# Two of seven quadrant products, done once more as seven products of quarters

## The chip, the cores and the metric

The kernel is written for one core of a Trainium2 chip. A core has a matrix engine (TensorE, PE in the profile; its weight loads are shown apart, as PEld), a vector engine (VectorE, DVE), an activation engine (ScalarE, ACT), a general engine (GpSimd, POOL), and SyncE (SP), whose queue issues most of the transfers between the chip's main memory and the core's memory. The engines run side by side, each in the order of its own queue, and wait for one another by semaphores. TensorE writes its results to PSUM, a small memory of banks; DVE and ACT read them from there. The metric is the device time of one execution, in microseconds; lower is better.

## The reference

The reference is four layers, one after the other, on eight 512x512 float32 matrices: a grid stencil, a transformer block with attention, a gated expert and a low-rank response. The change touches two feed-forward layers, that of the transformer block and that of the expert:

```python
# transformer block
h = _ln(x) * g2 + beta2
ff = _gelu2(h @ W1 + b1) @ W2 + b2
return x + ff
# expert
h = jax.nn.gelu(jnp.einsum('bsh,bhi->bsi', input_tensor, Wi_b) + bi_b[:, None, :], approximate=False)
o = jnp.einsum('bsi,bih->bsh', h, Wo_b) + bo_b[:, None, :]
r = o + input_tensor
```

For each of the eight matrices both are a product 512x512 by 512x2048, a GELU, and a product 512x2048 by 2048x512, whose result is added to the layer's input.

## The kernel before

The last stage, `mlp_stage` (L1237), runs 16 passes, q = 0 to 15: passes 0 to 7 are the transformer's feed-forward for the eight matrices, passes 8 to 15 the expert's. The hidden width of 2048 is cut into four groups g of 512, so a pass is four 512x512 products in its first layer and four, added up, in its second.

Each 512x512 product is cut into 2x2 quadrants of 256 and done by the Strassen-Winograd scheme: seven products of quadrants in place of eight, at the price of sums and differences of quadrants. For the first layer the sums of the weights are made by `w_quads` (L1573) and those of the input by `b_quads` (L1543). For the second layer the sums of the activations (left side) are made on DVE by `s13`, `t2s2`, `t4s4`, those of the weights wo (right side) on POOL by `t13` (L1738), `t2s2`, `t4s4`. A quadrant product of the second layer is `second` (L1672): for each of the four groups four matmuls that load 128x128 weights and stream 256 columns, all 16 added up in one PSUM bank.

The order is written out by hand. A pass has 56 steps of four matmuls each: steps 0 to 27 are the first layer (seven products for each group), steps 28 to 55 the second: p1 from step 28, p5 from 32, p2 from 36, p6 from 40, p3 from 44, p7 from 48, p4 from 52. A table `hooks` says which other work is issued before which step (`at`, L1958); `go(s)` inside `run` (L1599) issues it. Each engine keeps the order in which its work was issued. So a hook sets the place in every queue, not the time: an engine that is ahead does the work earlier than the step's matmuls, one that is behind does it later.

Hooks that matter here: the loads (`load_wi` L1406, `load_wo` L1419, `load_x`) on SP's queue; `w_quads` of groups 2 and 3 of the same pass at steps 7 and 14 and of groups 0 and 1 of the next at 46 and 50, on POOL; `add_row` (L1456), a 128x2048 addition on POOL at step 2; `norm` at 29 and `b_quads` of the next pass at 51, on DVE; in passes 0 to 7 four steps of a Gram-Schmidt loop (`gs_b`, L1313) at 4, 18, 40 and 53, each of which goes from DVE to POOL (a square root), back to DVE, and ends with two small transfers from POOL's queue (`gs_a`, L1302) that the next step waits for; in passes 9 to 15 the tail of the pass before (normalization, spread through main memory, response).

Buffers: a tile pool hands out a fixed number of buffers under each tag, in turn; a new tile waits until the last reader of the old one in its buffer is done. Tags x0 to x3 hold the first layer's weights (one buffer of 128x2048 each, one for each group), wo0 to wo3 those of the second layer, act0 to act3 the activations, and six PSUM banks (tag u) go round among all products. In pass 15, p4 is done in two halves by rows, each followed by `last_row` (L1873), with the last normalization between them.

Of the kernel before, what the change touches and what calls it, by code (L numbers as in the profile page):

```python
# [11 lines left out]
F32 = mybir.dt.float32  # L12
# [4 lines left out]
ALU = mybir.AluOpType  # L17
# [1219 lines left out]
def mlp_stage(tc, a, small, xp, io, wo8, x1d, ident, eidx, sigs, layernorm, rstd_of, phalf, wl3, g2, b1, first):  # L1237
# [19 lines left out]
    with ExitStack() as ctx:  # L1257
# [160 lines left out]

        def load_wo(q):  # L1419
            one = expert(q) if q >= NB else None  # L1420
            wos[q] = {}
            for g in range(NG):
                t = wp.tile([P, KC, D], F32, name=f"wo_{q}_{g}", tag=f"wo{g}", bufs=1)
                if q < NB:
                    load_w2(nc, t, a, g)
                else:
                    nc.sync.dma_start(
                        t,
                        a["Wo_e"][one, g * D : (g + 1) * D, :].rearrange(
                            "o (j p) d -> p (o j) d", p=P  # L1430
                        ),
                    )
                wos[q][g] = t

        def load_extra(q):

# [162 lines left out]
        def run(q, hooks):  # L1599
            def go(s):  # L1600
                for f in hooks.get(s, []):
                    f()

            func = AF.Gelu_apprx_sigmoid if q < NB else AF.Gelu
            bi = b1 if q < NB else extra[q][0]
            x = xs[q]
            acts, ss = {}, {}

            def act_quad(g, i, j):

                return acts[g][:, 2 * j : 2 * j + 2, H * i : H * i + H]

            def s13(g):
                ss[g] = io.tile([P, 2, H], F32, name=f"s_{q}_{g}", tag=f"v{g}", bufs=2)
                add(ss[g], act_quad(g, 1, 0), act_quad(g, 1, 1))
                add(act_quad(g, 1, 0), act_quad(g, 0, 0), act_quad(g, 1, 0), ALU.subtract)

            for g in range(NG):
                acts[g] = ap.tile([P, KC, D], F32, name=f"act_{q}_{g}", tag=f"act{g}", bufs=1)
                out = {  # L1620
                    (i, j): acts[g][:, 2 * i : 2 * i + 2, H * j : H * j + H]
                    for i in range(2) for j in range(2)
                }

                def gelu(i):
                    for k in (2 * i, 2 * i + 1):
                        j = 4 * g + k
                        pin(
                            nc.scalar.activation(  # L1629
                                acts[g][:, k, :], acts[g][:, k, :], func, bias=bi[:, j : j + 1]  # L1630
                            )
                        )

                p = []
                for m, (an, bn) in enumerate(L1):
                    go(7 * g + m)
                    A, B = wss[q, g][an], tbs[q][bn]
                    u = ps.tile([P, 2, H], F32, name=f"u_{q}_{g}_{m}", tag="u", bufs=6)
                    for i in range(2):
                        for k in range(2):  # L1640
                            mm(
                                as_rows(u, B(k))[i], A[:, k, i * P : (i + 1) * P], B(k),
                                i == 0 and k == 0, i == 1 and k == 1,
                            )
                    p.append(u)
                    if m == 0:
                        u1 = ap.tile([P, 2, H], F32, name=f"u1_{q}_{g}", tag="tmp", bufs=4)
                        pin(nc.scalar.copy(u1, p[0]))  # L1648
                    elif m == 1:
                        add(out[0, 0], p[1], u1)  # L1650
                    elif m == 2:
                        u2 = ap.tile([P, 2, H], F32, name=f"u2_{q}_{g}", tag="tmp", bufs=4)
                        add(u2, p[2], u1)
                        if g:
                            s13(g - 1)
                    elif m == 3:
                        u3 = ap.tile([P, 2, H], F32, name=f"u3_{q}_{g}", tag="tmp", bufs=4)
                        add(u3, p[3], u2)
                    elif m == 4:
                        add(out[1, 1], p[4], u3)  # L1660
                        add(u2, p[4], u2)
                    elif m == 5:
                        add(out[1, 0], p[5], u3)
                        gelu(1)
                    elif m == 6:
                        add(out[0, 1], p[6], u2)
                        gelu(0)

            wo, ts = wos[q], {}
            tvs = extra["t", q]  # L1670

            def second(s, A, B, each=None):  # L1672
                y = ps.tile([P, 2, H], F32, name=f"y_{q}_{s}", tag="u", bufs=6)
                for g in range(NG):
                    go(s + g)
                    if s == 28 and g == 2:
                        s13(NG - 1)
                    for i in range(2):
                        for m in range(2):
                            mm(  # L1680
                                y[:, m, :], A(g)[:, i, m * P : (m + 1) * P], B(g)[:, i, :],
                                g + i + m == 0, g + i + m == NG + 1,
                            )
                    if each:
                        each(g)
                return y

            def x_add(i, j, t):
                o = quad(x, i, j)
                add(o, t, o)  # L1690

            def b(i, j):
                return lambda g: quad(wo[g], i, j)

            yu = ap.tile([P, 2, H], F32, name=f"yu_{q}", tag="yu", bufs=1)

            def t2s2(g):
                gadd(tvs[g], quad(wo[g], 1, 1), tvs[g], ALU.subtract)
                add(ss[g], ss[g], act_quad(g, 0, 0), ALU.subtract)

            def t4s4(g):
                gadd(quad(wo[g], 1, 0), quad(wo[g], 1, 0), tvs[g], ALU.subtract)
                add(act_quad(g, 0, 1), act_quad(g, 0, 1), ss[g], ALU.subtract)

            p1 = second(28, lambda g: act_quad(g, 0, 0), b(0, 0))
            pin(nc.scalar.copy(yu, p1))
            x_add(0, 0, p1)
            p5 = second(32, lambda g: ss[g], lambda g: tvs[g], t2s2)
            x_add(1, 1, p5)
            x_add(0, 1, p5)  # L1710
            p2 = second(36, lambda g: act_quad(g, 0, 1), b(1, 0), t4s4)
            x_add(0, 0, p2)
            p6 = second(40, lambda g: ss[g], lambda g: tvs[g])
            add(yu, p6, yu)
            x_add(0, 1, yu)
            p3 = second(44, lambda g: act_quad(g, 0, 1), b(1, 1))
            x_add(0, 1, p3)
            p7 = second(48, lambda g: act_quad(g, 1, 0), b(0, 1))
            add(yu, p7, yu)
            x_add(1, 1, yu)  # L1720
            x_add(1, 0, yu)
            if q < NQ - 1:
                p4 = second(52, lambda g: act_quad(g, 1, 1), b(1, 0))
                x_add(1, 0, p4)
            else:
                for m in range(2):
                    y = ps.tile([P, H], F32, name=f"y_{q}_52_{m}", tag="u", bufs=6)
                    for g in range(NG):
                        if g % 2 == 0:
                            go(52 + 2 * m + g // 2)  # L1730
                        for i in range(2):
                            mm(
                                y, act_quad(g, 1, 1)[:, i, m * P : (m + 1) * P],
                                b(1, 0)(g)[:, i, :], g + i == 0, g + i == NG,
                            )
                    last_row(m, y)

        def t13(q, g):  # L1738

            w = wos[q][g]  # L1740
            t = io.tile([P, 2, H], F32, name=f"t_{q}_{g}", tag=f"v{g}", bufs=2)
            gadd(t, quad(w, 0, 1), quad(w, 0, 0), ALU.subtract)
            gadd(quad(w, 0, 1), quad(w, 1, 1), quad(w, 0, 1), ALU.subtract)
            extra.setdefault(("t", q), {})[g] = t
# [223 lines left out]
        for q in range(NQ):  # L1968
            hooks = {}
            nx = q + 1 if q + 1 < NQ else None  # L1970

            at(hooks, 0, load_wo, q)
            if nx:
                if nx >= NB:
                    at(hooks, 45, load_extra, nx)
                at(hooks, 2, load_x, nx)
                for g in range(NG):
                    at(hooks, 7 * (g + 1), load_wi, nx, g)
            if 1 <= q <= NB:
                at(hooks, 4, lambda q=q: nc.sync.dma_start(x2d[q - 1], xs[q - 1]))  # L1980

# [5 lines left out]
            if nx:  # L1987
# [9 lines left out]
                        at(hooks, 46 + c, scale, nx, c)  # L1997
                at(hooks, 51, b_quads, nx)
                at(hooks, 46, w_quads, nx, 0, gadd)
                at(hooks, 50, w_quads, nx, 1, gadd)  # L2000
            if q < NB:
                for i, s in enumerate((4, 18, 40, 53) if q else (18, 24, 40, 53)):
                    at(hooks, s, gs_b, 4 * q + i)
# [118 lines left out]
```

## Time and profile before

| what | us |
|---|---|
| median of three runs | 2673.83 (2673.12 to 2674.03) |
| the profiled execution's own time | 2672.99 |
| its span, first to last instruction | 2671.2 |
| PE busy | 2629.2 |
| DVE busy | 1879.8 |
| POOL busy | 1484.6 |
| ACT busy | 1008.3 |

The page is one execution under the profiler. Busy time is the union of an engine's instructions; the difference of span and busy time is when it stood still. A group is a line of the kernel, an engine, an operation, the tiles written and read (out<-in), shapes and a count. L1265 is the helper `mm`, through which every matmul of the last stage goes, so groups there are told apart by their tiles: u are the products of the first layer, y those of the second. The last stage begins at 1075.7 us and ends with the span; its passes 1 to 7 start 96.69 us apart, passes 9 to 14 about 100.3 to 100.9.

### The profile page before, as it was taken

The page shows a single profiled execution, that of the slowest core. Times are in us where ns is not written, and L with a number is a line of the kernel's source. Part 1 is how long each engine was busy: PE and PEld are TensorE (multiplying, and loading weights), DVE is VectorE, ACT ScalarE, POOL GpSimd, SP SyncE. Part 2 cuts the span into 40 slices and gives each one's busy share as a digit, 9 for nine tenths or more (in the row PEclk, how much of TensorE's full clock was granted, in tenths as well). Part 3 has the DMA queues.
Part 4 walks back from the last instruction along what each step waited for, and adds up shares of the span by engine and source line. Part 5 has one row for each costly group of instructions (what it writes and reads, how often), then busy time and mean ns, then how long its engine had stood idle before and what let it go on. Part 6 is the DMA issues. An engine that isn't in the chain of part 4 may idle for free.

```text
span 2671.2 us, 39378 instructions
## 1 busy us (share of the span) xinstructions
PE 2629.2 (98%) x14152; PEld 1950.0 (73%) x14152; DVE 1879.8 (70%) x3436; ACT 1008.3 (38%) x2100; POOL 1484.6 (56%) x1099
## 2 busy tenths in 40 slices
PE   6999999999999999999999999999999999999998
PEld 3455555555555555888888888888888888888887
DVE  7978888888888656666656656666466676676675
ACT  2676767677777765211211211210111221221221
POOL 4556565556555664565556565655635545545543
PEclk9999999999999999999999999999999999999999
DMA  9775766666666554653454454445345445445331
GB/s 332 251 233 191 249 214 228 214 244 236 202 239 218 189 167 151 197 148 98 149 148 133 134 145 151 111 141 163 107 140 172 138 151 178 136 149 181 123 105 37
DMA packets 241817, 460.31 MB, mean 172 GB/s; under 512 B 33905, under 2 KB 77497, under 8 KB 232535
## 3 DMA queue, kind: packets, MB, share of 16 engines
q1 hardware_dynamic: 237754, 447.04, 49.4%
q0 software_dynamic: 3552, 10.72, 3.0%
q8 instruction: 113, 1.85, 0.3%
q14 instruction: 82, 0.66, 0.1%
q10 hardware_dynamic: 316, 0.03, 0.0%
HBM read 398.43 MB, written 55.09 MB: 170 GB/s over the span
## 4 chain that ended last, share of the span: by engine, by line
PE 94%; DVE 3%; DMA 1%; ACT 1%; SPq 0%; issue 0%; POOL 0%; DVEq 0%; POOLq 0%; ACTq 0%
PE u L1265 29%; PE y L1265 28%; PE tr L593 9%; PE s L590 6%; PE ctx L590 4%; PE o L590 4%; PE pv L590 4%; PE pk L590 4%; PE pq L590 4%; PE xtr L593 1%; PE xb L593 1%; DMA a<-in_A 0%; DMA bt<-td 0%; DVE bt L1058 0%; PE po L1265 0%
## 5 line engine op out<-in xcount | busy, mean ns | idle before, releaser
L1034 POOL TENSOR_TENSOR bt<-bt,mk 128x1024 f32<-128x1024 f32 x256 | 541.9, 2141 | 56.8 <-DMA bt<-in_bias 45.6
L1265 PE MATMUL y<-wo,act 128*128 128x256 f32 x2560 | 566.3, 380 | 0.0
L1265 PEld LDWEIGHTS y<-wo,act 128*128 128x128 f32 x2560 | 484.5, 190 | 71.6 <-issue 6.7
L1063 ACT ACTIVATE bt<-bt,mn 128x512 f32<-128x512 f32 x512 | 365.8, 718 | 77.7 <-DVE mn L1058 77.6
L593 PEld LDWEIGHTS tr<-ident,bt 128*128 128x128 f32 x2048 | 229.3, 141 | 149.3 <-issue 102.1
L1058 DVE CUSTOM_DVE_ANT_0 bt<-s,bt 128x512 f32<-128x512 f32 x512 | 329.9, 684 | 4.9 <-PE s L590 4.3
L1265 PE MATMUL u<-bt,wi 128*128 128x256 f32 x1440 | 330.5, 379 | 0.0
L1271 DVE TENSOR_TENSOR act<-u,u 128x512 f32<-128x512 f32 x256 | 173.1, 683 | 200.7 <-PE u L1265 132.5
L1265 PEld LDWEIGHTS u<-bt,wi 128*128 128x128 f32 x1440 | 273.5, 190 | 37.2
L1090 ACT COPY pt<-tr 128x512 f32<-128x512 f32 x376 | 207.9, 585 | 207.0 <-PE tr L593 199.2
L593 PE MATMUL tr<-ident,bt 128*128 128x128 f32 x2048 | 276.2, 277 | 7.7 <-ACT pt L1090 3.3
L1265 PE MATMUL u<-tb,ws 128*128 128x256 f32 x1024 | 242.2, 379 | 0.0
L1265 PE MATMUL y<-t,s 128*128 128x256 f32 x1024 | 227.8, 380 | 0.0
L1274 POOL TENSOR_TENSOR t<-wo,t 128x512 f32<-128x512 f32 x64 | 107.4, 1702 | 203.0 <-PE y L1265 203.0
L1265 PEld LDWEIGHTS u<-tb,ws 128*128 128x128 f32 x1024 | 194.3, 190 | 26.6 <-DVE tb L1271 0.2
L1265 PEld LDWEIGHTS y<-t,s 128*128 128x128 f32 x1024 | 194.0, 190 | 26.1
L1629 ACT ACTIVATE act<-act,b 128x512 f32<-128x512 f32 x128 | 82.9, 711 | 292.8 <-DVE act L1271 292.8
L1088 DVE COPY pt<-tr 128x512 f32<-128x512 f32 x136 | 93.7, 689 | 139.8 <-PE tr L593 139.3
L1629 ACT ACTIVATE act<-act,bi 128x512 f32<-128x512 f32 x128 | 83.8, 712 | 282.6 <-DVE act L1271 282.6
L1648 ACT COPY u<-u 128x512 f32<-128x512 f32 x64 | 36.4, 569 | 397.0 <-PE u L1265 275.9
L1271 DVE TENSOR_TENSOR x<-y,x 128x512 f32<-128x512 f32 (+1 forms) x97 | 64.7, 680 | 155.1 <-PE y L1265 104.7
L1271 DVE TENSOR_TENSOR u<-u,u 128x512 f32<-128x512 f32 x192 | 130.9, 682 | 55.4 <-PE u L1265 55.2
(331 smaller groups left out, 4179.8 us busy)
## 6 DMA issues: line engine op xcount, KB each, us to landing
bt<-in_bias SPq DMA_DIRECT2D x256, 512.0 KB
wo<-in_W SPq DMA_DIRECT2D x32, 1024.0 KB
wi<-in_Wi SPq DMA_DIRECT2D x32, 1024.0 KB
wo<-in_Wo_e SPq DMA_DIRECT2D x32, 1024.0 KB
wi<-in_W SPq DMA_DIRECT2D x28, 1024.0 KB
td<-tt SPq DMA_DIRECT2D x22, 1024.0 KB
bt<-td SPq DMA_DIRECT2D x176, 128.0 KB
gq<-coef_q SPq DMA_DIRECT2D x21, 512.0 KB
```

The costliest lines, as they stand in the source:

```text
L590: pin(nc.tensor.matmul(out, lhsT=lhsT, rhs=rhs, start=start, stop=stop))
L593: pin(nc.tensor.transpose(out, src, ident))
L1034: nc.gpsimd.tensor_tensor(bt, bt, mask[b, r][:, None, :].to_broadcast([P, 2, S]), ALU.add)
L1058: nc.vector.tensor_tensor_reduce(bt[:, i, :], ss[h], bt[:, i, :], -1.0, 3.0e38, ALU.add, ALU.min, mn)
L1063: nc.scalar.activation(bt[:, i, :], bt[:, i, :], AF.Exp, bias=mn, scale=-1.0, accum_out=sums[b, c][:, h, r : r + 1],)
L1088: pin(nc.vector.tensor_copy(pt[:, :, r % 2, :], tr))
L1090: pin(nc.scalar.copy(pt[:, :, r % 2, :], tr))
L1265: pin(nc.tensor.matmul(out, lhsT=lhsT, rhs=rhs, start=start, stop=stop))
L1271: pin(nc.vector.tensor_tensor(out, x, y, op))
L1274: pin(nc.gpsimd.tensor_tensor(out, x, y, op))
L1629: nc.scalar.activation(acts[g][:, k, :], acts[g][:, k, :], func, bias=bi[:, j : j + 1])
L1648: pin(nc.scalar.copy(u1, p[0]))
```

## The change

The products p7 and p4 of the second layer are cut once more. Each is, over the four groups, a product of 256x1024 by 1024x256; its operands are seen as 2x2 quarters of 128 (with the groups side by side as a third dimension), and the same scheme is used on the quarters: seven products of quarters, each four matmuls (one for each group) that load 128x128 and stream 128 columns. `quarters` sets up the operands and their sums: four left sums on DVE, four right sums on POOL, 128x512 each, one of each in place and three of each in new homes. `third` issues the 28 matmuls into two PSUM banks, four products in the first and three in the second, and adds the products up: one copy on ACT and three sums on DVE after the first bank, one sum after the second, into a tile in the core's memory that then stands where the PSUM bank of p7 or p4 stood. In pass 15 only p7 is cut.

The homes of the sums are the buffers x1, x2 and x3, in which the first layer's weights of groups 1 to 3 are no longer needed from step 28 on. They are in use until the end of p7 (x1) and p4 (x2, x3), so the loads of the next pass move: group 0 at step 21 (was 7), group 1 at step 52 (was 14), groups 2 and 3 at step 0 of the next pass, ahead of its `load_wo` (were 21 and 28). `w_quads` of group 1 moves from step 50 to step 1 of the next pass. The right sums of p7 are at steps 28 to 31, its left sums at 40 to 43; the left sums of p4 at 44 to 47, its right sums at 41 to 44 (from pass 9 on all at step 40). The four activation tiles become one, and the four wo tiles become one, so that a quarter of all four groups can be taken with one access.

```diff
         def load_wo(q):
-            wos[q] = {}
+            wos[q] = wp.tile([P, NG, KC, D], F32, name=f"wo_{q}", tag="wo", bufs=1)
             for g in range(NG):
-                t = wp.tile([P, KC, D], F32, name=f"wo_{q}_{g}", tag=f"wo{g}", bufs=1)
+                t = wos[q][:, g]
...
+            acts = ap.tile([P, NG, KC, D], F32, name=f"act_{q}", tag="act", bufs=1)
...
+            def quarters(key, i, j, wi_, wj, homes):
+                def left(k, m):
+                    o = H * i + P * m
+                    return acts[:, :, 2 * j + k, o : o + P]
+                def right(k, n):
+                    o = H * wj + P * n
+                    return wo[:, :, 2 * wi_ + k, o : o + P]
+                s1, s2, s4, t1, t2, t4 = homes
+                L, M = left, right
+                four[key] = dict(
+                    a=((L(0, 0), M(0, 0)), (s2, t2), (L(0, 1), M(0, 1)), (s1, t1)),
+                    b=((L(1, 0), M(1, 0)), (s4, M(1, 1)), (L(1, 1), t4)),
+                )
+                sub = ALU.subtract
+                of_left = [
+                    lambda: add(s1, L(0, 1), L(1, 1)), lambda: add(s2, s1, L(0, 0), sub),
+                    lambda: add(L(0, 1), L(0, 0), L(0, 1), sub), lambda: add(s4, L(1, 0), s2, sub),
+                ]
+                of_right = [
+                    lambda: gadd(t1, M(0, 1), M(0, 0), sub), lambda: gadd(M(0, 1), M(1, 1), M(0, 1), sub),
+                    lambda: gadd(t2, M(1, 1), t1, sub), lambda: gadd(t4, M(1, 0), t2, sub),
+                ]
+                return of_left, of_right
+            def quarter_homes(n):
+                for k in range(1, 4)[n:]:
+                    t = xp.tile([P, KC, D], F32, name=f"q4_{q}_{k}", tag=f"x{k}", bufs=1)
+                    homes[k] = [t[:, c, :].rearrange("p (g d) -> p g d", g=NG) for c in range(KC)]
+            def third(s, key):
+                jobs = [
+                    (n, k, g, v) for n in "ab" for k, v in enumerate(four[key][n]) for g in range(NG)
+                ]
+                ys = {
+                    n: ps.tile([P, 4, P], F32, name=f"y_{q}_{s}{n}", tag="u", bufs=6) for n in "ab"
+                }
+                w = ap.tile([P, 4, P], F32, name=f"yw_{q}_{s}", tag="tmp", bufs=4)
+                y = ys["a"]
+                for i, (n, k, g, (A, B)) in enumerate(jobs):
+                    if i % 7 == 0:
+                        go(s + i // 7)
+                    last = len(four[key][n]) - 1
+                    mm(
+                        ys[n][:, k, :], A[:, g, :], B[:, g, :], k + g == 0,
+                        k == last and g == NG - 1,
+                    )
+                    if n == "a" and k == last and g == NG - 1:
+                        pin(nc.scalar.copy(w[:, 0, :], y[:, 0, :]))
+                        add(w[:, 1, :], y[:, 1, :], w[:, 0, :])
+                        add(w[:, 2, :], y[:, 2, :], w[:, 1, :])
+                        add(w[:, 1:4:2, :], y[:, 3:4, :].to_broadcast([P, 2, P]), w[:, 1:3, :])
+                add(w[:, 0:3, :], ys["b"][:, 0:3, :], w[:, 0:3, :])
+                return w.rearrange("p (m n) d -> p m (n d)", m=2)
...
+            l7, r7, l4, r4 = early_quarters()
+            for i, f in enumerate(r7):
+                at(hooks, 28 + i, f)
+            for i, f in enumerate(l7):
+                at(hooks, 40 + i, f)
+            if q < NQ - 1:
+                for i, f in enumerate(l4):
+                    at(hooks, 44 + i, f)
+                for i, f in enumerate(r4):
+                    at(hooks, 41 + i if q <= NB else 40, f)
...
-            p7 = second(48, lambda g: act_quad(g, 1, 0), b(0, 1))
+            p7 = third(48, "p7")
...
-                p4 = second(52, lambda g: act_quad(g, 1, 1), b(1, 0))
+                p4 = third(52, "p4")
...
+            if q:
+                at(hooks, 0, load_wi, q, 2)
+                at(hooks, 0, load_wi, q, 3)
+                at(hooks, 1, w_quads, q, 1, gadd)
             at(hooks, 0, load_wo, q)
...
-                for g in range(NG):
-                    at(hooks, 7 * (g + 1), load_wi, nx, g)
+                at(hooks, 21, load_wi, nx, 0)
+                at(hooks, 52, load_wi, nx, 1)
...
-                at(hooks, 50, w_quads, nx, 1, gadd)
```

More of the change, by code (lines that the diff above doesn't have):

```diff
@@ L1432, in load_wo @@
                     )
-                wos[q][g] = t
         def load_extra(q):
@@ L1606, in run @@
             x = xs[q]
-            acts, ss = {}, {}
+            ss = {}
+            acts = ap.tile([P, NG, KC, D], F32, name=f"act_{q}", tag="act", bufs=1)
             def act_quad(g, i, j):
-                return acts[g][:, 2 * j : 2 * j + 2, H * i : H * i + H]
+                return acts[:, g, 2 * j : 2 * j + 2, H * i : H * i + H]
             def s13(g):
@@ L1618, in run @@
             for g in range(NG):
-                acts[g] = ap.tile([P, KC, D], F32, name=f"act_{q}_{g}", tag=f"act{g}", bufs=1)
                 out = {
-                    (i, j): acts[g][:, 2 * i : 2 * i + 2, H * j : H * j + H]
+                    (i, j): acts[:, g, 2 * i : 2 * i + 2, H * j : H * j + H]
                     for i in range(2) for j in range(2)
@@ L1629, in gelu @@
                             nc.scalar.activation(
-                                acts[g][:, k, :], acts[g][:, k, :], func, bias=bi[:, j : j + 1]
+                                acts[:, g, k, :], acts[:, g, k, :], func, bias=bi[:, j : j + 1]
                             )
@@ new lines, in run @@
+            four = {}
+            homes = {}
+            def quarter_homes(n):
[26 more added lines that the diff above has]
+                return w.rearrange("p (m n) d -> p m (n d)", m=2)
@@ L1688, in x_add, with early_quarters @@
+            def early_quarters():
+                quarter_homes(0)
+                h1, h2, h3 = (homes[k] for k in (1, 2, 3))
+                return (
+                    quarters("p7", 1, 0, 0, 1, (h1[3], h2[0], h2[1], h1[0], h1[1], h1[2]))
+                    + quarters("p4", 1, 1, 1, 0, (h3[1], h3[2], h3[3], h2[2], h2[3], h3[0]))
+                )
             def x_add(i, j, t):
@@ L1692, in b @@
             def b(i, j):
-                return lambda g: quad(wo[g], i, j)
+                return lambda g: quad(wo[:, g], i, j)
             yu = ap.tile([P, 2, H], F32, name=f"yu_{q}", tag="yu", bufs=1)
             def t2s2(g):
-                gadd(tvs[g], quad(wo[g], 1, 1), tvs[g], ALU.subtract)
+                gadd(tvs[g], quad(wo[:, g], 1, 1), tvs[g], ALU.subtract)
                 add(ss[g], ss[g], act_quad(g, 0, 0), ALU.subtract)
             def t4s4(g):
-                gadd(quad(wo[g], 1, 0), quad(wo[g], 1, 0), tvs[g], ALU.subtract)
+                gadd(quad(wo[:, g], 1, 0), quad(wo[:, g], 1, 0), tvs[g], ALU.subtract)
                 add(act_quad(g, 0, 1), act_quad(g, 0, 1), ss[g], ALU.subtract)
+            l7, r7, l4, r4 = early_quarters()
[8 more added lines that the diff above has]
+                    at(hooks, 41 + i if q <= NB else 40, f)
             p1 = second(28, lambda g: act_quad(g, 0, 0), b(0, 0))
@@ L1738, in t13 @@
         def t13(q, g):
-            w = wos[q][g]
+            w = wos[q][:, g]
             t = io.tile([P, 2, H], F32, name=f"t_{q}_{g}", tag=f"v{g}", bufs=2)
```

## The prediction

> **What bounds the kernel now.** I read the page first (shares of engines, slices, the chain that ended last), then a table of stretches cut at pass borders of the feed-forward stage, then PE's timeline at places that show what a narrow matmul costs, then POOL's and DVE's timeline around one pass border.
>
> The page:
>
> ```profile
> PE 2629.2 (98%) x14152; PEld 1950.0 (73%) x14152; DVE 1879.8 (70%) x3436; ACT 1008.3 (38%) x2100; POOL 1484.6 (56%) x1099
> PEclk9999999999999999999999999999999999999999
> PE 94%; DVE 3%; DMA 1%; ACT 1%; SPq 0%; issue 0%; POOL 0%; DVEq 0%; POOLq 0%; ACTq 0%
> ```
>
> PE carries 94% of the chain. The same for stretches: the first two are passes 5 and 6 (of 0 to 15), the third and fourth passes 11 and 12, the last is pass 15 with the end of the kernel.
>
> ```profile
> 1559.52:1656.21 96.69, 96.69 (x449) 85.12 (x448) 62.16 (x113) 18.78 (x29) 56.82 (x47) 1.00 0.45 136
> 1656.21:1752.90 96.69, 96.69 (x449) 85.12 (x448) 61.21 (x113) 18.78 (x29) 57.27 (x47) 1.00 0.47 137
> 2150.20:2250.85 100.65, 100.50 (x500) 87.14 (x499) 66.51 (x94) 19.27 (x32) 54.24 (x35) 1.00 0.48 155
> 2250.85:2351.13 100.28, 100.28 (x499) 87.19 (x498) 66.68 (x94) 19.27 (x32) 54.71 (x35) 1.00 0.47 155
> 2552.14:2671.20 119.06, 110.94 (x581) 93.45 (x579) 71.24 (x107) 24.66 (x51) 43.65 (x29) 0.96 0.20 71
> ```
>
> After length come busy PE, weight loads (PEld), DVE, ACT, POOL. Passes 5 and 6 are PE without a hole: 448 instructions in 96.69 us, one per 215.8 ns. An f32 matmul shows as two instructions, each with its own weight load; I call one a half. So a half less is time less, and what counts is what a half of 128 columns costs. Four places of the timeline bear on it (start, length of the group, count):
>
> ```profile
> 1499.95 1.05 PEld L1265 LDWEIGHTS u<-bt,wi 128*128 128x128 f32 x5
> 2018.18 0.86 PEld L1265 LDWEIGHTS pg<-pool,gw 128*128 128x128 f32 x7
> 1885.85 0.85 PEld L1265 LDWEIGHTS pw<-hmat,qm 32*128 32x128 f32 x7
> 482.74 0.69 PEld L593 LDWEIGHTS tr<-ident,bt 128*128 128x128 f32 x6
> ```
>
> Less the last load's own length (190 ns; 187 for pw, 141 for tr) and divided by the steps between, the spacing is 215 ns at 256 columns streamed, 112 ns at one column (pg), 110 ns at 32 (pw), 110 ns for transposes that load 128 columns and stream 128 (tr). One column and 32 cost the same: the spacing there is the load's, and the stream lies beside it.
>
> **The change part by part.**
>
> Matmuls. A quadrant product has 16 matmuls of 256 columns, 32 halves: 32 x 0.2158 = 6.91 us. As quarters it has 7 x 4 = 28 of 128 columns, 56 halves. Bounds for a half: below, the stream alone, half of 0.216, 0.108; above, load and stream in turn, 0.112 + 0.108 = 0.220. I take 0.112, the longer of the two side by side, because tr, the nearest row, does both in 110 ns; what speaks against is that tr is a transpose with a shorter load (141 against 190 ns). So 56 x 0.112 = 6.27 us, 0.635 less (bounds 0.86 less, 5.4 more). There are 31 such products: p7 in 16 passes, p4 in 15. Passes 0 to 14 save 30 x 0.635 = 19.05 us.
>
> The Trainium skill, "TensorE: Matmul & The Clock Gate", section "Back-to-back issue gap", speaks against this: it says that in a stream of loads and matmuls the spacing is set by both, about 81 ns at 128 columns where streaming alone would give about 56. An estimate by that page adds its 25 ns to the 110 of tr, 135 ns a half, 7.56 us a product, and the 31 products would be 20 us slower instead of 20 faster. The tr row, 110 ns with both, doesn't show it; no f32 matmul of this shape is in the trace.
>
> Pass 15. Only p7 is cut, and PE there waits for normalized rows from DVE (busy 110.94 of 119.06), so the 0.6 us may go into that wait: 0 to 0.6, I take 0.2 less.
>
> Passes 9 to 14. Pass 12 is 100.28, pass 11 100.65: PE waits a little for ACT's scaled columns at step 38. SP's queue is freed of the load of wi group 3 at step 28, which stands ahead of the tail's spread. By PE's timeline passes 9, 11 and 13 are 0.6, 0.4 and 0.4 us longer than pass 12: 0 to 1.4 less, I take 0.7.
>
> DVE. New per pass: 8 subtractions or sums of 128x512 on activations (0.69 us alone, about 1.0 beside POOL), and per quartered product one ACT copy and four DVE sums (128, 128, 256 and 384 columns: about 0.28, 0.28, 0.42, 0.55) in place of none. That is about 8.6 us on 62 of 95. It fits; what matters is order. b_quads (hook 51) used to run at step 48.5; now it stands behind the sums of p7's first bank, which PE completes at step 50. Behind b_quads stand p7's other sums, and behind those the Gram-Schmidt step of hook 53. On POOL, w_quads of group 1 now comes at step 1 of a pass, ahead of add_row and of the square root that Gram-Schmidt step 4 waits for in DVE's queue. Before, this border was:
>
> ```profile
> 1651.44 0.68 DVE L1291 CUSTOM_DVE_ANT_0 junk_gn<-qb 64x512 f32<-64x512 f32 x1
> 1654.05 0.74 DVE L1322 SCALAR_TENSOR_TENSOR qm<-qb,al,qm 64x512 f32<-64x512 f32 x1
> ...
> 1667.79 0.67 DVE L1271 TENSOR_TENSOR u<-u,u 128x512 f32<-128x512 f32 x1
> ```
>
> ```profile
> 1655.09 1.03 POOL L1307 DMA_DIRECT2D qb<-qm  x2 [1.93 <-DVE qm L1322]
> 1656.14 4.54 POOL L1274 TENSOR_TENSOR x<-x,b2row 128x2048 f32<-128x2048 f32 x1
> 1664.68 0.94 POOL L1296 TENSOR_TENSOR gs_d<-gn_s,phalf 64x1 f32<-64x1 f32 x1 [4.01 <-DVE gn_s L1291]
> ```
>
> After, by the same rows: p3 ends at 1642.4, p7's first bank at 1646.2, its sums at 1647.6, b_quads 2.9 us, 1650.5; p7's rest 2.4, 1652.9; Gram-Schmidt 3.35, 1656.3; POOL's two DMAs 1657.6; four w_quads operations 5.4, 1663.0; add_row 4.54, 1667.6; the root 0.94, 1668.5; DVE's rest of the step 1.64 and two sums 1.25, 1671.4. These sums free the PSUM bank of product 4 of the new pass. Six banks go round, so PE wants it for product 10, at 1654.94 + 17.26 = 1672.2. The spare time falls from 5.0 us to 0.8. Beside POOL single DVE operations take 1.3 to 1.5 us instead of 0.42 or 0.69, so it can go 1.5 us over. Seven passes (1 to 7) have this: 0 to 10 us more, I take 2.
>
> Costed at nothing, with the cover named. POOL: 8 more subtractions (1.28 to 1.7 us, 10 to 14 us on 57 of 95). Those for p7 stand at steps 28 to 31, where POOL idled from step 26 to 33, are ready by about 34 and wanted at 48; those for p4 come after step 41, end at about 47, wanted at 53. They push w_quads of group 0 to about 51, wanted at 58. In passes 9 to 14 they push add_beta by 5 us, and with it the first sum into x that frees a bank for p7's second bank: wanted at step 50, ready at about 48.9. If this cover goes, each us late is a us of PE. Loads: group 1 of the next pass is issued when p7 ends (about 1648.7) and needs some 5 us (1 MB is 3 at the 343 to 369 GB/s that stretches at pass borders show, and I allow 2 to start), POOL is ready for it at 1657.6. Groups 2 and 3 are now ahead of wo at step 0: 6 MB, 17 us, so the last wo lands at step 11 and POOL starts on it at step 15. SP waits in order on these, but only wo and x loads stand behind, which had to wait for p4 anyway. One tile instead of four for the activations and wo makes the first write wait for p4's last read; the first products of the next pass come later than that in PE's own order.
>
> Sum: -19.05 - 0.2 - 0.7 + 2 = -17.95. The profiled execution took 2672.99 (span 2671.2), so 2655.0; the median of the runs, 2673.83, is 0.84 above it, so 2656.
>
> **The rivals.**
>
> Loads don't hide (slower): a half of 128 columns costs clearly more than 112 ns, at every quartered product. It decides from 6.91 / 56 = 123 ns on. If a quarter of the stream's 108 ns shows, a half costs 139 ns, a product 7.78: 31 x 0.88 = 27 more, with the small terms 2702; at the bound of 220, 31 x 5.4 = 167, 2842. For it: loads of 190 ns in the rows where 128x128 f32 weights are used, and no such stream in the trace. Against it: pg issues such loads every 112 ns, pw shows 32 columns at no extra, tr 128 at none.
>
> DVE and POOL come late at step 10 (no change): 2 to 4 us of PE in each of seven passes, 14 to 28 us against the 20 gained, 2668 to 2682, most likely 2673. For it: only 0.8 us spare by my reckoning, and longer DVE operations beside POOL. Against it: PE catches up nothing, but DVE does, as it has 30% idle right after, and with w_quads of group 1 moved away POOL is idle while b_quads runs.
>
> **How the numbers follow.** My forecast has 0.77, late DVE 0.11, loads that don't hide 0.12. The forecast's own range: with a half of 0.108, no waits and both small terms whole, 2646; with 0.114 and 10 us of waits, 2667. To leave out no more than 2 in 10 the range goes up into the second case: 2646 to 2674. 0.2% of 2673.8 is 5.3 us, about what a measurement of this kernel can tell. Below 2668.5 lies nearly all of the forecast: faster 0.77; same 0.09, mostly from late DVE; slower 0.14.
>
> **What would show it.** Loads of the new tiles in groups that give a spacing of 112 ns, and a quartered product of 6.3 us from first to last matmul. Passes 1 to 7 of 95.4 us with PE busy without a hole; a hole at product 10 released by DVE means the second rival. Passes 9 to 14 near 99. The forecast is wrong if the spacing is above 115 ns, if a hole of over 1 us stands at step 10 or between p7 and p4, or if pass 15 grows because p7's longer sums delay its last rows.

## The result, and the profile after

The changed kernel takes 2704.98 us (median of 4 runs, 2704.63 to 2706.51), the kernel before 2673.93 in the same session: a ratio of 1.0117, with a 95% interval of 1.01 to 1.0135. It is 1.2% slower. The forecast was 2656, its range ended at 2674.

The page of the profiled execution (span 2702.8 us, own time 2704.63):

```profile
PE 2623.1 (97%) x14896; PEld 1965.1 (73%) x14896; DVE 2158.8 (80%) x3684; ACT 1013.2 (37%) x2131; POOL 1696.5 (63%) x1223
PE 74%; DVE 9%; POOL 9%; issue 4%; DMA 2%; SPq 0%; ACT 0%; POOLq 0%; DVEq 0%; ACTq 0%
```

PE works 6 us less than before, but carries only 74% of the chain instead of 94%: DVE and POOL together now hold 18% of it. DVE is busy 279 us longer, POOL 212. The same stretches as before the change (passes 5, 6, 11, 12, and 15 with the end):

```profile
1574.28:1674.03 99.75, 97.29 (x499) 86.61 (x498) 84.01 (x130) 19.20 (x31) 71.12 (x54) 0.98 0.45 133
1674.03:1772.10 98.07, 95.62 (x499) 85.38 (x497) 83.12 (x130) 19.19 (x31) 71.26 (x54) 1.00 0.45 134
2174.84:2276.50 101.66, 99.25 (x549) 87.62 (x547) 79.53 (x106) 19.47 (x34) 67.34 (x43) 1.00 0.45 151
2276.50:2379.69 103.19, 100.77 (x548) 89.14 (x547) 82.25 (x115) 19.48 (x34) 69.17 (x44) 0.98 0.44 153
2584.52:2702.80 118.28, 110.28 (x606) 93.82 (x604) 80.79 (x116) 24.81 (x52) 58.21 (x38) 0.96 0.25 89
```

Length and busy PE (the first two numbers) were equal in passes 5 and 6 before; now PE has a hole of 2.5 us in each of these passes. Who ends the holes, and how much of a pass the narrow products take, is in two views, the waits of PE and PE's loads in the timeline of pass 5:

```profile
PE u L1265 <- DVE u L1271: 18.9, 7, 4.1
PE y_48b L1265 <- DVE x L1936: 14.5, 6, 2.4
```

```profile
1664.09 0.97 PEld L1265 LDWEIGHTS y_48a<-q 128*128 128x128 f32 x8
1664.98 0.97 PEld L1265 LDWEIGHTS y_48b<-wo,act 128*128 128x128 f32 x8
```

Eight loads of y_48a start 0.89 us before the next eight; over all groups of y_48a a half comes every 111.6 ns. So the matmuls do what was forecast, and the time is lost in two kinds of holes, one of them in each of these passes (pass 1 has a further one of 1.4 us, at product 4). Seven are at product 10 of passes 1 to 7, ended by the sum that frees a PSUM bank. Six are in passes 9 to 14 ahead of the second bank of p7 (y_48b), ended by the tail sum into x, which frees that bank. Against passes without a hole (95.39 and 98.98 us, measured below), passes 1 to 7 have 28.4 us too much, 9 to 14 20.7, pass 0 1.3: 50.4 us, against some 22 gained. The remaining 2.9 us of the difference lie ahead of the stage, which begins at 1078.6 instead of 1075.7 in this profile; it began between 1075.3 and 1080.6 in the kernels below, whatever their change.

Why DVE is late is read at a border, here from pass 4 to 5 (border at 1574.28). DVE, then POOL:

```profile
1556.04 1.96 DVE L1271 TENSOR_TENSOR act<-act 128x512 f32<-128x512 f32 x1
1563.06 1.65 DVE L1271 TENSOR_TENSOR q<-q,act 128x512 f32<-128x512 f32 x1
1568.59 1.06 DVE L1271 TENSOR_TENSOR yw<-y_48a,yw 128x128 f32<-128x128 f32 x3
...
1585.62 4.54 DVE L1291 CUSTOM_DVE_ANT_0 junk_gn<-qb 64x512 f32<-64x512 f32 x1 [2.09 <-DMA qb<-qm]
1593.35 0.67 DVE L1271 TENSOR_TENSOR u<-u,u 128x512 f32<-128x512 f32 x1
```

```profile
1559.08 3.40 POOL L1274 TENSOR_TENSOR q<-wo,q 128x512 f32<-128x512 f32 x2
1585.10 4.51 POOL L1274 TENSOR_TENSOR x<-x,b2row 128x2048 f32<-128x2048 f32 x1
1590.25 0.94 POOL L1296 TENSOR_TENSOR gs_d<-gn_s,phalf 64x1 f32<-64x1 f32 x1 [0.64 <-DVE gn_s L1291]
```

Left sums of 128x512 that take 0.68 us alone take 1.65 to 1.96 while POOL works on p4's right sums and on the weight sums of group 0 of the next pass. The norm of the Gram-Schmidt step (L1291) takes 4.54; at this place before the change, where the border was at 1559.52, it took 0.67:

```profile
1567.23 0.67 DVE L1291 CUSTOM_DVE_ANT_0 junk_gn<-qb 64x512 f32<-64x512 f32 x1
```

The long one starts 0.52 us after the row sum on POOL and ends 0.55 after it. The sum that frees product 4's bank then ends at 1594.0, and PE starts product 10 at 1594.17, 2.46 us after it could have.

### The profile page after: what moved, and what is told of

It is laid out like the page before. It is cut to its first block, busy times and chain, and to the rows that moved or that the text cites. A ratio compares the mean times of both kernels' runs of the same rounds, so it can differ in the third digit from the quotient of the medians.

```text
span 2702.8 us, 41335 instructions
## 1 busy us (share of the span) xinstructions
PE 2623.1 (97%) x14896; PEld 1965.1 (73%) x14896; DVE 2158.8 (80%) x3684; ACT 1013.2 (37%) x2131; POOL 1696.5 (63%) x1223
## 4 chain that ended last, share of the span: by engine, by line
PE 74%; DVE 9%; POOL 9%; issue 4%; DMA 2%; SPq 0%; ACT 0%; POOLq 0%; DVEq 0%; ACTq 0%
PE u L1265 24%; PE y L1265 11%; PE tr L593 9%; PE s L590 5%; PE ctx L590 4%; PE pv L590 4%; PE o L590 4%; PE pk L590 4%; PE pq L590 4%; POOL ws L1274 2%; DVE act L1271 2%; DVE q L1271 2%; POOL q L1274 1%; POOL wo L1274 1%; POOL x L1274 1%
## 5 line engine op out<-in xcount | busy, mean ns | idle before, releaser
L1265 PE MATMUL u<-bt,wi 128*128 128x256 f32 x1440 | 337.4, 385 | 18.9 <-DVE u L1271 18.9
L1265 PE MATMUL y<-wo,act 128*128 128x256 f32 x1568 | 352.1, 380 | 0.0
L1265 PEld LDWEIGHTS y<-wo,act 128*128 128x128 f32 x1568 | 296.1, 190 | 46.0 <-issue 6.7
L590 PE MATMUL s<-kt,qt 32*128 32x512 f32 x1024 | 165.9, 640 | 1.0 <-ACT kt L681 0.8
L1271 DVE TENSOR_TENSOR act<-act 128x512 f32<-128x512 f32 x95 | 134.3, 1414 | 2.2
```

Source lines behind the costliest of these rows:

```text
L590: pin(nc.tensor.matmul(out, lhsT=lhsT, rhs=rhs, start=start, stop=stop))
L1265: pin(nc.tensor.matmul(out, lhsT=lhsT, rhs=rhs, start=start, stop=stop))
L1271: pin(nc.vector.tensor_tensor(out, x, y, op))
```

## The experiments

Ratios are to the kernel before, from runs on the same chip, with 95% intervals.

**What makes the holes: sums, moves or matmuls.** The first three leave operand sums out, the fourth undoes the quartering and keeps the moves.

```
e1, e2:  s1, s2, s4 = L(0,1), L(0,0), L(1,0);  of_left = []
e1, e3:  t1, t2, t4 = M(0,1), M(1,1), M(1,0);  of_right = []
e4:      p7 = second(48, ...); p4 = second(52, ...); no quarters
```

> All sixteen operand sums of the two quartered products are left out, the left ones on DVE and the right ones on POOL (the products then take unsummed operands, so the results are other numbers). The narrow matmuls, the sums of their banks and the moved loads stay. If the operand sums are what makes DVE late (theory), the holes of 2.8 us at product 10 of passes 1 to 7 and of 2.7 us before the second bank of p7 in passes 9 to 14 go, passes 1 to 7 take 95.4 us and 9 to 14 about 99, and the time is 2674 - 20 = 2654, at most 2660. If the moved work on POOL or the moved loads make the holes (rival 1), they stay, 2685 to 2705. If the narrow matmuls cost more than they look (rival 2), the time stays above 2674 with no holes.

> Only the eight left sums (DVE) are left out, the right ones on POOL stay; results are other numbers. They take 11 to 13 us of DVE in a pass of after, mostly at 1.65 to 1.96 us each. Theory (left sums and POOL block each other): DVE comes to the bank sums of p7 some 10 us earlier, the holes go, 2654 to 2664. Rival (POOL's longer queue alone makes the root and the beta sum late): the holes stay at over half their size, 2685 to 2700.

> Only the eight right sums (POOL) are left out, the left ones on DVE stay; results are other numbers. Theory: those left sums that no longer stand beside POOL fall from about 1.75 to 0.69 us, w_quads still meets some of them, most of both holes goes: 2658 to 2678. Rival (the plain amount of DVE's new work, 0.69 us each, makes it late, POOL or not): the holes stay at over half, 2688 to 2700.

> Both products as before the change, undivided; only the moves stay (loads of groups 1 to 3 later, the sums of group 1 at step 1 on POOL, single tiles). Theory: at the border POOL's four operations of 1.28 us and the row sum stand ahead of the root, which eats the 5.0 us that were spare, so a hole of 0 to 1 us in passes 1 to 7: 2672 to 2681. Rival 1 (the moves make the loss): 2690 to 2705, and the 50 us of waits are there without any quartered product.

Measured: without any operand sums (e1) 2652.8 us (0.9919, 0.9902 to 0.9936), without the left ones (e2) 2657.5 (0.9938, 0.9921 to 0.9954), without the right ones (e3) 2652.6 (0.9917, 0.99 to 0.9933), moves alone (e4) 2671.9 (0.9991, 0.9982 to 1.0001). In e1 passes 1 to 7 take 95.4 us (one 95.58), 9 to 14 98.98, PE without a hole. In e2 and e3 all holes of passes 0 to 14 are gone but one at product 10 of pass 1 (2.9 and 0.9 us). With the moves alone passes 1 to 7 are 96.69 as before, and 9 to 14 all 100.29, which is 1.4 us less in sum.

So neither the narrow matmuls nor the moves cost anything, and neither the left sums nor the right sums alone make PE wait, but for that one hole of pass 1: only both together do. The stretch of 34 us from step 31 to p7's second bank, at the border from pass 3 to 4, shows it: without left sums, without right sums, and with both (after length come busy PE, PEld, DVE, ACT, POOL):

```profile
1419.70:1453.70 34.00, 34.00 (x177) 30.41 (x176) 24.03 (x31) 6.71 (x10) 29.21 (x23) 1.00 0.28 66
```

```profile
1415.96:1449.95 33.99, 33.99 (x177) 30.40 (x176) 26.76 (x39) 6.70 (x10) 21.56 (x16) 1.00 0.28 67
```

```profile
1433.72:1467.72 34.00, 34.00 (x177) 30.41 (x176) 31.25 (x37) 6.70 (x10) 29.17 (x21) 1.00 0.27 66
```

DVE is busy 24.0 and 26.8 us of the 34, and 31.3 with both. In the two kernels without one side, DVE ends the sums of p7's first bank 7.3 us ahead of the border, in the changed kernel 4.6, which is 2.7 us later. The chain behind hands this on link by link: without left sums the Gram-Schmidt step ends 1.4 us after the border, the row sum 12.7, and product 4's bank is free at 17.1; in the changed kernel these are 4.1, 15.3 and 19.7. PE wants the bank at 17.3, so 2.5 of the 2.7 us are the hole.

**Is it the amount of work on DVE, or POOL beside it?** All right sums on DVE (gadd becomes add):

> After, with the eight right sums on DVE instead of POOL at the same steps. Theory (DVE and POOL block each other, so a sum on POOL costs DVE nearly as much as doing it): at steps 40 to 47 DVE has 12 sums of 0.69 us and perhaps four to six of them longer by 1.06 beside the sums of group 0, 12.6 to 14.7 us against some 13 now. The holes of passes 1 to 7 stay within 1.5 us of 2.8, those of 9 to 14 shrink as the beta sum comes 5 us earlier on POOL: 2680 to 2705. Rival (the plain amount of DVE's work makes it late): four more sums at 0.69 us in that stretch are 2.8 us more in each of 13 passes, 2705 + 36 = 2741 (2725 to 2745).

Measured 2689.3 us (e12; 1.0056, 1.0039 to 1.0072), 16 us faster than with these sums on POOL. The page:

```profile
PE 2622.8 (98%) x14896; PEld 1963.5 (73%) x14896; DVE 2167.3 (81%) x3808; ACT 1013.0 (38%) x2131; POOL 1509.1 (56%) x1099
```

DVE does 124 operations more and is busy only 8.5 us longer, while alone they would be 124 x 0.69 = 86; POOL is relieved of 187 us. Holes at product 10 are 2.0 us (3.5 in pass 1), those of passes 9 to 14 0.4 (1.4 in pass 9), and pass 0 has a new one of 4.6. So a sum on POOL costs DVE nearly what it would cost to do it itself, by these figures 77 of 86 us.

**Undoing the two waits by order alone.** Three kernels move work and leave none out; a fourth, e8, quarters p7 only.

```
e5:  add_row at 26 (was 2) and Gram-Schmidt at 6, 18, 40, 53 (was 4, 18, 40, 53), passes 1 to 7
e6:  l7 and l4 at 31 (were 40 to 43, 44 to 47), passes 9 to 15
e7:  e5 + e6
e8:  p4 = second(52, ...); p7's sums in the homes of groups 2 and 3; load and sums of group 1 as before
```

> After, with two moves in the order of work: in passes 1 to 7 the Gram-Schmidt step of hook 4 goes to hook 6, and in passes 1 to 7 the row sum on POOL (4.5 us) goes from hook 2 to hook 26, where POOL is idle. Theory: the first norm of that step (4.29 us long, beside the row sum) falls to 0.7 us and the sums that free product 4's bank go ahead of it, so the hole at product 10 goes: seven passes less 3 to 4.4 us each, 2705 - 28 = 2677 (2674 to 2682), passes 9 to 14 as in after. Rival (DVE is late by its own sums, wherever that step stands): the hole stays or moves to product 12, 2692 to 2705.

> After, with the eight left sums of passes 9 to 15 at step 31, where POOL is idle in these passes, instead of steps 40 to 47. Passes 0 to 8 as in after. Theory: each takes 0.69 us instead of 1.2 to 5.0, none waits for the beta sum on POOL, the bank for p7's second half is free in time: six passes less 2.7 to 4.3 us each, 2705 - 20 = 2685 (2682 to 2690). Rival (the beta sum itself comes too late on POOL, 5 us behind p4's right sums): the hole stays at over half, 2694 to 2705.

> The moves of the last two kernels together. Theory: the holes are two separate ones, the gains add: 2705 - 28 - 20 = 2657 (2652 to 2668), faster than before the change. Rival (the clock or the port takes part of it back): 2668 to 2690.

> Only p7 in quarters, p4 undivided; its sums lie in the homes of groups 2 and 3, so the load and the sums of group 1 stay where they were before the change. 16 products less 0.65 us each: 10 us less matmuls. Theory: DVE has four left sums and no p4 bank sums, POOL four right sums at steps 28 to 31 and nothing of group 1 at the border, so the spare time at product 10 is near its old 5 us: 2664 to 2668. Rival (any operand sums beside POOL make DVE late): holes stay at over 1 us, 2675 to 2690.

Measured: e5 2677.05 us (1.001, 1.0 to 1.002), e6 2689.9 (1.0056, 1.0039 to 1.0073), e7 2659.3 (0.9948, 0.9932 to 0.9965) and e8 2661.4 (0.995, 0.9934 to 0.9967). Against the changed kernel e5 removes 28 us, e6 15, both together 46. The group of the norm in the changed kernel and in e5:

```profile
L1291 DVE CUSTOM_DVE_ANT_0 junk_gn<-qb 64x512 f32<-64x512 f32 x32 | 47.8, 1494 | 15.8 <-DMA qb<-qm 15.8
```

```profile
L1291 DVE CUSTOM_DVE_ANT_0 junk_gn<-qb 64x512 f32<-64x512 f32 x32 | 22.1, 691 | 3.2 <-DMA qb<-qm 3.1
```

Away from the row sum the 32 norms take 0.69 us in the mean, and passes 2 to 7 are 95.39, though the left sums are as long as ever and DVE comes as late to the border. So here order decides: the lateness has nothing to hit. Whether the step's move or the row sum's was the one that did it is not shown, as no kernel makes one alone. In passes 9 to 14 of the changed kernel a left sum begins 0.50 us after the beta sum (`add_beta`, 128x2048) on POOL and ends 0.54 after it; the tail sum that frees the bank comes behind. DVE, then POOL:

```profile
2255.05 5.00 DVE L1271 TENSOR_TENSOR q<-act,q 128x512 f32<-128x512 f32 x1
2266.67 0.74 DVE L1936 SCALAR_TENSOR_TENSOR x<-po,st,x 128x512 f32<-128x512 f32 x1
```

```profile
2254.55 4.96 POOL L1274 TENSOR_TENSOR x<-x,beta 128x2048 f32<-128x2048 f32 x1
```

At step 31 POOL is idle in these passes, and the same sums take 0.69 us (timeline of e6). But eight of them in a row make the gate's small sums late, a new wait of PE:

```profile
2221.57 0.69 DVE L1271 TENSOR_TENSOR q<-q,act 128x512 f32<-128x512 f32 x1
2222.78 0.68 DVE L1271 TENSOR_TENSOR q<-act,q 128x512 f32<-128x512 f32 x1
```

```profile
PE pz L1265 <- DVE h L1907: 3.4, 4, 1.3
```

This is why e6 lands at the upper end of what was expected. p7 alone (e8) has no hole at product 10 and gains 11.2 us in passes 0 to 14 (9.8 of matmuls, 1.4 of ACT's wait in passes 9, 11 and 13, as with the moves alone), more than expected.

**Does it help passes 1 to 8 to have p7's left sums early?**

```
e9:   l7 at 31 in passes 1 to 8, all else as changed
e14:  e9 + r4 at 40 + Gram-Schmidt at 4, 18, 44, 53
```

> After, with p7's four left sums of passes 1 to 8 at step 31 instead of 40 to 43; the Gram-Schmidt step and the row sum stay where after has them. In after these four take 5.1 us (0.68, 0.69, 1.96, 1.75) and DVE comes to the sums of p7's first bank 2.8 us later than without right or without left sums, the same 2.8 us that the hole has. Theory (lateness carried through the border): the 2.8 us go, product 10 is just met, passes 1 to 7 take 95.4 us again: 2677 (2674 to 2684). Rival (the order of the Gram-Schmidt step and the row sum alone makes the hole, or the lateness only moves to steps 31 to 40): 2692 to 2705.

> As the kernel with p7's left sums at step 31 in passes 1 to 8, with p4's right sums on POOL at step 40 at once and the Gram-Schmidt step of hook 40 at hook 44 behind them. In the former POOL waited for the norm of that step, which came 3.4 us later on DVE, and so p4's right sums and the sums of group 0 ran late, beside p4's left sums and b_quads (4.1 us instead of 2.9). Theory (DVE and POOL make each other late through that root): POOL's eight operations run 8 us earlier, DVE is at the sums of p7's first bank in time, holes at product 10 under 1 us: 2674 to 2690. Rival (steps 31 to 40 have no room on DVE whatever POOL does): holes of 3 to 4 us stay, 2705 to 2725.

Measured: e9 2722.4 us (1.0175, 1.0158 to 1.0192), slower than the changed kernel and outside both expectations, and e14 2707.8 (1.0119, 1.0103 to 1.0134), where the rival put it. The waits of PE in e9:

```profile
PE u L1265 <- DVE u L1271: 28.0, 7, 4.1
PE u L1265 <- DVE yw L1271: 3.6, 4, 1.4
```

At step 31 of these passes POOL is in p7's right sums and then in the right sums of `t2s2` and `t4s4`, so p7's left sums take 1.64 to 1.76 us there too. They make the Gram-Schmidt step of hook 40 3.4 us late, POOL waits for its norm with p4's right sums and group 0 behind it, and these then run beside p4's left sums and b_quads. With POOL freed of that wait e14 gains 15 us back, but holes of 2.9 us remain: in this order DVE has no room between step 31 and the border at either place that was tried for p7's left sums. My theory that moving half of the left sums would give the lateness back fell.

**A version that beats the kernel before and the changed one.** The order of e5, with p7's left sums at step 31 in all passes (e10), in pass 0 and 9 to 15 (e11), in 9 to 15 (e13); p4's stay at 44 to 47.

```
at(hooks, 31 if q > NB else 40 + i, f)      # e13; e10: 31; e11: q == 0 or q > NB
```

> The later Gram-Schmidt step and row sum in passes 1 to 7, and p7's left sums at step 31 in all passes, p4's at 44 to 47 as in after. Theory: DVE has 10 us less ahead of the beta sum and the tail sums in passes 9 to 14, enough for p7's second bank, and without p4's sums at step 31 the 0.7 us hole before the gate's product goes: passes 9 to 14 at 98.98. Passes 0 and 1 lose part of their 1.4 us: 2653 to 2657. Rival (p4's left sums beside the beta sum still make the tail sums late): 2660 to 2675.

> As the kernel before it in this list, but p7's left sums at step 31 only in pass 0 and passes 9 to 15, at 40 to 43 in passes 1 to 8. Theory: the same within 2 us, since passes 1 to 8 were without a hole with these sums at 40: 2653 to 2657. If steps 31 to 40 have no room on DVE in passes 1 to 7, this one is the faster.

> The later Gram-Schmidt step and row sum in passes 1 to 7, and p7's left sums at step 31 in passes 9 to 15 alone. Theory: passes 1 to 8 as in the kernel with both moves (95.4 and 98.1), 9 to 14 as in the two kernels with p7's sums early (98.98 each, no hole before the gate's product), and pass 1 without the 2.9 us hole at step 4 that those two have: some 3 to 4 us less than 2659, 2654 to 2658. Rival (it is the same as its neighbours within what their runs differ): 2658 to 2662.

Measured: e10 2658.3 (0.9932, 0.9915 to 0.9949), e11 2659.0 (0.9937, 0.9921 to 0.9954) and e13 2654.5 us (0.9924, 0.991 to 0.9937). The first two lie 1 to 2 us above their expectation. They have a hole of 2.9 us in pass 1 at step 4 (product 4 waits there), which the early sums in pass 0 make worse (1.4 in e13), and pass 1 is 3.2 and 4.4 us longer than in e13. In e13 passes 2 to 7 are 95.39, 9 to 14 98.98:

```profile
PE 2608.3 (98%) x14896; PEld 1954.2 (74%) x14896; DVE 2117.4 (80%) x3684; ACT 1015.0 (38%) x2131; POOL 1696.3 (64%) x1223
PE 91%; DVE 3%; DMA 2%; POOL 2%; issue 1%; ACT 0%; SPq 0%; DVEq 0%; POOLq 0%; ACTq 0%
```

DVE and POOL do all the sums of the changed kernel, and with another order they cost PE almost nothing. It is 0.8% faster than before the change (2675.5 beside it), and within 1.5 us of the forecast that failed for the order as it was.

## Why the prediction was wrong

**Matmuls: right.** 112 ns a half was forecast, 111.6 is measured. Passes 1 to 7 without sums are 1.30 us shorter than before, 0.65 a product against 0.635. The rival "loads don't hide" is out, and with it the spacing that the Trainium skill's page "TensorE: Matmul & The Clock Gate", section "Back-to-back issue gap", would have given (135 ns by the estimate).

**Pass 15: open.** It is 0.78 us shorter here, forecast 0.2, bound 0.6. But it is 118.0 to 119.2 us in all kernels that quarter p7, and 118.5 with the moves alone against 119.07 before, so one profile of each does not tell 0.2 us. **Passes 9 to 14, ACT's wait: right,** 1.4 less with the moves alone, the upper bound; 0.7 was taken.

**DVE: the step that failed.** The term "+2 (0 to 10)" for passes 1 to 7 measured 28.4 us. The chain itself was reckoned well. The kernel without left sums (e2) follows it: first bank's sums done 7.3 us ahead of the border (forecast 7.3), Gram-Schmidt done 1.4 after it (1.4), row sum done at 12.7 (12.7), bank free at 17.1 (16.5), wanted at 17.26. It broke at its input, "8 subtractions or sums of 128x512 on activations (0.69 us alone, about 1.0 beside POOL)", of which the 8.6 us a pass take the lower price (8 x 0.69 and twice 1.53), and at taking DVE to be free when PE completes p7's first bank. The groups of the three tile forms q give 70.6 + 40.5 + 36.5 us for 93 sums; the 31 in place are the difference of the group act from act in the changed kernel and without left sums, 134.3 - 79.4 = 54.9. That is 202.5 us for 124 sums, 1.63 each. "It fits" (8.6 us on 62 of 95) was reckoned over the pass, while DVE was busy 31.3 of the 34 us from step 31 to p7's second bank, and in the last 37 us ahead of the border stood still for 0.8 us in all. With 0.8 us spare, and each us late a us of PE, 2.7 us of lateness were enough. The row beside POOL that I had, 1.3 to 1.5 us for single operations, was in the prediction, but taken as a spread and not as the price.

The norm beside the row sum I did not price at all. In the kernel without left sums it took 4.23 us, which made the root wait until 0.6 us after the row sum and so used up 0.6 of the 0.8 us spare; the chain stayed in time only because the root stands behind the row sum on POOL anyway. In the changed kernel it is a link of the late chain.

**Costed at nothing: the cover named for add_beta was gone.** "Wanted at step 50, ready at about 48.9": PE stood still for 2.4 us there, and the six passes are 20.7 us too long in sum, with the slower clock behind three of these holes. The 5 us by which p4's right sums push the beta sum were reckoned; that the left sums stand still beside it for 5.0 us, and go on at 1.75 beside group 0, was not. The loads and the tiles were rightly costed at nothing, and so nearly was POOL's own amount: with the right sums alone (e2) one hole of 2.9 us is left, in pass 1.

**The rival "DVE and POOL come late at step 10"** named the mechanism, place and size for passes 1 to 7 (14 to 28 us, measured 28.4). That the size agrees at its end is in part luck: 20.3 of the 28.4 us are holes, and most of the rest is a slower clock behind them, which neither the forecast nor the rival had. The rival had 0.11, and its outcome was put at "no change" because the same lateness in passes 9 to 14 was not added to it. What was said against it, that DVE catches up "as it has 30% idle right after", was no argument: the hole comes before the idle time.

The Trainium skill, "SBUF — State Buffer", section "Who interferes with whom", states that a DVE instruction with two SBUF inputs contends with a GpSimd instruction that reads SBUF, over a shared port pair that is an exclusive lock; that the lock is held for the whole instruction it says of DVE's two-port modes. The trace agrees with a wait of that length: norm and left sum of 4.54 and 5.00 us end 0.55 and 0.54 us after the operation of POOL that they started behind, near their own 0.68. An estimate by that rule is that a left sum beside back-to-back subtractions of POOL waits for one of them, 1.28 us, and takes up to 1.96; measured are 1.65 to 1.96 there and 1.63 in the mean over all, so it would have priced the term far nearer than 1.0. What the runs show is that the two engines' sums stretch each other (POOL's subtraction of 1.28 us takes 1.6 to 1.7 beside DVE's); by which part of the chip, no run here tells apart.

## What to carry to other kernels

A sum moved to POOL is not off DVE: beside SBUF operations on POOL price DVE's by the timeline's rows with POOL busy, here 1.6 to 2 us instead of 0.69 (and as long as the POOL operation where that is a wide one), and not by their time alone. Look for idle time of DVE in the stretch ahead of the deadline and not over the whole pass, and put wide POOL operations where DVE has only PSUM work or none (sums with one input from PSUM, x<-y,x, took 0.68 us in the mean beside POOL too, 55 cases in the changed kernel). Before giving up a change that made holes, see which single wait each hole ends on: moving the row sum, one Gram-Schmidt step and the left sums of the last passes (e7) brought back 46 of 50 us here.

## What the runs showed of the hardware that was not expected

The granted clock falls after holes of only 2.0 to 2.9 us, and not after each of them. After the hole of pass 5, PE's timeline and the stretch behind it, and the same stretch of pass 6:

```profile
1594.17 3.63 PE L1265 MATMUL u<-bt,wi 128*128 128x256 f32 x8 [2.46 <-DVE u L1271]
1597.63 1.89 PE L1265 MATMUL u<-tb,ws 128*128 128x256 f32 x8
```

```profile
1593.80:1597.20 3.40, 3.03 (x7) 2.52 (x8) 1.42 (x3) 2.55 (x5) 3.31 (x4) 0.55 1.16 289
1693.90:1697.30 3.40, 3.40 (x16) 3.01 (x17) 1.05 (x2) 2.91 (x5) 3.31 (x3) 1.00 1.13 284
```

Eight halves take 3.46 us to the next group instead of 1.73, at a clock of 0.55. The equal hole of pass 6 is followed by full speed. Passes 3, 5, 7, 10, 12 and 14 have this and are 1.5 to 1.7 us longer than their neighbours; with pass 1, behind its hole of 4.1 us, that is some 11 of the 50 us lost. Over passes 0 to 14 of all the kernels here, the clock fell to about 0.5 after none of 22 holes of 0.7 to 1.43 us, after 30 of 51 holes of 2.04 to 2.95 us, and after all 12 holes of 3.52 us or more. The Trainium skill, "TensorE: Matmul & The Clock Gate", section "HAM oscillation — how this bites in real kernels", gives no idle gaps above some 3.4 us as the rule; here shorter ones were enough in more than half of the cases.
